# A group-normalised convolution with two kinds of image: where half products, sums and their transfers stand

## The chip, the core and the metric

The kernel runs on one core of a Trainium2 chip. The metric is the device time of one execution in microseconds; the number compared is the median over runs. The core has five engines with queues of their own that work in order: TensorE (PE: matmuls, PEld: its weight loads), VectorE (DVE), ScalarE (ACT), GpSimd (POOL) and SyncE (SP, which only issues transfers). Transfers run on 16 DMA engines; those that SP issues are plain loads and stores, those that POOL issues here add to what lies at their destination.

## The reference

The input `x` holds 160 images of 128 channels and 32 x 32 pixels, the weights `U` are 5 rows of 147456 numbers. What is computed, cut to what matters:

```python
def reference(x, L0_conv_U):
    def _L0_conv_ref(x, U):                       # N = 5 weight sets, 3 x 3 taps, padding 1
        s1 = (jnp.max(U) - jnp.min(U)) / 3.0
        v1 = s1 * floor(U / s1)
        s2 = s1 / 5.0
        v2 = s2 * floor((U - v1) / s2)
        w = (v1 + v2).reshape(128 * 5, 128, 3, 3)
        xb = x.reshape(B // 5, 5 * C, H, W)
        act = conv_general_dilated(xb, w, ..., feature_group_count=5)
        return act.reshape(...)
    def _gn(v, G=32, eps=1e-5):                   # 4 neighbouring channels form a group
        m, s = mean and variance of a group in one image
        return (v - m) / sqrt(s + eps)
    return x + _L0_conv_ref(_gn(x), L0_conv_U)
```

So each image is normalised by group of channels, convolved with one of five quantised 3 x 3 kernels, and added to itself. 32 images share a weight set.

## The kernel before

**Images and loops.** The 128 channels lie on the 128 partitions, so an image is a tile of 128 x 1024 f32 (512 KB). Two images form a chunk (`xt`), one load or one store of 1 MB. `Main.run` has one loop over the 160 images, and the order in which Python emits instructions is the order of every engine's queue (`tc.manual_schedule()`): nothing is reordered afterwards. In iteration `i` the convolution of image `i` is emitted, and beside it work for neighbouring images: statistics for image `i + 14`, normalised parts for `i + 2` to `i + 4`, the result of `i - 1`, the store of `i - 2` and loads that run up to 17 images ahead.

**Statistics.** `measure` makes two passes of ACT over an image: `image_sum` (L187) adds its values up, `image_square` (L196) adds up the squares of its deviations, with the negative mean as its bias. Between them POOL turns the sum into the negative mean `minus` (L189) and the mean in `mv` (L190), and after the second pass into the variance in `mv` (L199). Groups of eight images (smaller ones at the start) then share two small matmuls that average over channels (`means`, L205, and `variances`, L220), with POOL's arithmetic between (`deviations`, L213 to L217) and after them (`deviation` and `scales`, L226 to L238), which ends in `rstd`, `shift` and `twice`. The two matmuls are emitted by `on_the_way`, from inside the convolution of the two images after the one whose measuring completed the group.

**Two kinds of image.** The normalised image goes to PE as a sum of two f16 parts. A *plain* image has `z` (ACT, L486), its high part `hi` (ACT, L494) and the rest `lo` (DVE, L543). The high part is convolved tap by tap: 18 matmuls with up to 512 columns (`taps`, L583). For the low part pairs of rows are combined first (DVE, L556 to L559, tile `rows`), which needs fewer products: 12 matmuls of about 256 columns into `eo` and 6 of about 512 into `m` (`product`, L619). A *combined* image (every third one, `i % 3 == 2`, from 14 on, 48 in all) combines rows before it is split: DVE and POOL make `v` (`combine`, L515 to L525), ACT its high part `vh` (L530), DVE the low part `vl` (L536), and both go through `product` alone.

**From products to result.** `m` holds half products of pairs of rows, `eo` the rest, each in PSUM; there are two buffers for `eo` and one for `m`. `leave` (ACT, L667) copies `m` out, to `mm` (f16) for a plain image and to `mw` (f32) for a combined one. `pairs` (DVE, L679 and L680) makes the sum and the difference of the halves: for a plain image in a tile `pq` of its own, for a combined image in a tile of the pool `sums`, which has three buffers. `residual` (DVE) adds `eo`: L703 writes a new tile of `sums` for a plain image, L699 adds to the tile that `pairs` has already taken for a combined one; it also frees the buffer of `eo`. `accumulate` (POOL, L716) then issues the transfer that adds the sum to the image in `xt`, in SBUF, and after it SP issues the store (L721). A buffer of `sums` is free again when that transfer has landed.

**Order within iteration `i`.** PE: the six matmuls for `m` come first, or after the first of the three columns of taps where image `i - 1` is combined (`late`); `on_the_way` stands ahead of the last column. DVE: `low_combined(i + 1)`, `combine(i + 2)`, `residual(i - 1)`, `pairs(i)`, then `low_part(i + 2)` and `combinations(i + 2)`, and in 21 of the 32 iterations of each of the first four sets two steps of `make_column`, which builds the next set's weights. ACT: `normalise`, first pass, `leave(i)`, `high_part` or `high_combined`, second pass. POOL: its part of `combine`, the small operations of the statistics, and `accumulate(i - 1)` at the iteration's end. SP: the store of a finished chunk and then the loads, in order; a chunk's place is one of 11 (`xpool`).

## Time and profile before

| what | value |
|---|---|
| median of 3 runs | 1152.48 us (1145.69, 1152.48, 1153.7) |
| the profiled execution's own time | 1146.97 us |
| its span (first to last instruction) | 1145.2 us |
| mean granted TensorE clock | 0.975 of full speed |
| instructions | 16411 |
| DMA | 254.45 MB, mean 222 GB/s |
| accumulating transfers (`xt<-sum`) | 153 of 512 KB, median 7.1 us from issue to landing |

How to read it: the profile is one execution, in microseconds from the span's start. A row of the waits says which engine sat idle at which line, what ended the idle time, for how long in total, how often, and at most. The chain of waits follows the last instruction back, at each step to what released it. Lines such as L679 are lines of the kernel before. Tiles are named without their buffer's number, so `sum` stands for all buffers of that pool. In the kernel with the change every line below the first edit has moved by five or so (L679 is L684 there).

### The profile page before, as it was taken

The numbers are of one execution on the slowest core, as the hardware profiler recorded it, in microseconds if no ns is written. First come the engines' busy times: TensorE is split into PE (matmuls) and PEld (weight loads), VectorE is DVE, ScalarE is ACT, GpSimd is POOL, SyncE is SP. The second block draws the span as 40 slices with busy tenths as digits, with TensorE's granted clock in tenths as the row PEclk, the third lists the DMA queues.
The fourth block names the chain that finished last, engine by engine and source line by source line (L and its number), as shares of the span: only waits on it lengthen the run. The fifth ranks groups of instructions, "written<-read, shape, count | busy, mean of one in ns | idle before, by whom it ended". The sixth has DMA issues, their size and how long they took to land.

```text
span 1145.2 us, 16411 instructions
## 1 busy us (share of the span) xinstructions
PE 1023.7 (89%) x5910; PEld 582.4 (51%) x5910; DVE 962.7 (84%) x1363; ACT 841.9 (74%) x1137; POOL 596.4 (52%) x965
## 2 busy tenths in 40 slices
PE   1999797999889989898889999989988999998997
PEld 0455454555554546455446455545554555555554
DVE  7996698978788989787988977889978988877886
ACT  4799776778768868688677767777867887786541
POOL 4644555474456556555556565536555655463420
PEclk9999999999998999999989999999999999999999
DMA  9348697888997897899788889888879789987773
GB/s 364 127 133 243 158 237 205 221 228 230 269 251 199 222 254 202 224 264 239 217 221 221 221 227 244 226 211 237 232 208 237 223 237 243 249 247 202 180 202 132
DMA packets 67290, 254.45 MB, mean 222 GB/s; under 512 B 5248, under 2 KB 5248, under 8 KB 67200
## 3 DMA queue, kind: packets, MB, share of 16 engines
q1 hardware_dynamic: 45168, 173.09, 44.1%
q0 software_dynamic: 22032, 80.23, 36.7%
q8 instruction: 48, 0.79, 0.3%
q14 instruction: 42, 0.34, 0.1%
HBM read 89.19 MB, written 83.89 MB: 151 GB/s over the span
## 4 chain that ended last, share of the span: by engine, by line
ACT 21%; DMA 18%; POOL 18%; PE 17%; DVE 13%; issue 12%; SPq 0%; POOLq 0%; DVEq 0%; ACTq 0%
DMA xt<-sum 15%; PE eo L583 8%; ACT junk L187 4%; ACT vh L530 4%; PE m L619 4%; ACT junk L196 4%; PE eo L619 4%; ACT z L486 4%; DMA xt<-in_x_dram 3%; POOL mv L199 3%; POOL v L516 3%; POOL rstd L229 2%; POOL xt L716 2%; DVE lo L543 2%; ACT hi L494 2%
## 5 line engine op out<-in xcount | busy, mean ns | idle before, releaser
L583 PE MATMUL eo<-hi,wt 128*128 128x496 f16 (+3 forms) x1998 | 497.1, 387 | 57.4 <-DVE sum L699 55.9
L619 PEld LDWEIGHTS <-wt 128*128 128x128 f16 x3690 | 363.2, 99 | 253.5 <-issue 31.7
L583 PEld LDWEIGHTS <-wt 128*128 128x128 f16 x2070 | 206.9, 101 | 266.1 <-issue 83.9
L199 POOL TENSOR_SCALAR mv<-squares 128x1 f32<-128x1 f32 x157 | 105.3, 671 | 324.6 <-ACT junk L196 323.0
L530 ACT ACTIVATE vh<-v,rstd 128x2048 f16<-128x2048 f32 x48 | 96.1, 2002 | 148.6 <-DVE v L525 100.3
L619 PE MATMUL eo<-rows,wt 128*128 128x248 f16 (+1 forms) x1308 | 201.6, 278 | 0.0
L196 ACT ACTIVATE junk<-xt,minus 128x1024 f16<-128x1024 f32 x157 | 179.8, 1146 | 13.9 <-POOL minus L189 12.3
L187 ACT ACTIVATE junk<-xt 128x1024 f16<-128x1024 f32 x157 | 164.7, 1049 | 34.1 <-DMA xt<-in_x_dram 32.6
L619 PE MATMUL m<-rows,wt 128*128 128x496 f16 (+1 forms) x654 | 159.6, 380 | 18.6 <-ACT mm L667 7.1
L716 POOL DMA_DIRECT2D xt<-sum x153 | 137.8, 903 | 40.7 <-DVE sum L699 19.1
L486 ACT ACTIVATE z<-xt,shift,rstd 128x1024 f32<-128x1024 f32 x112 | 137.9, 1231 | 25.5 <-POOL shift L236 25.5
L667 ACT ACTIVATE mm<-m 128x1024 f16<-128x1024 f32 x109 | 110.1, 1010 | 47.8 <-PE m L619 47.7
L543 DVE TENSOR_TENSOR lo<-z,hi 128x1024 f16<-128x1024 f32 x112 | 136.6, 1220 | 1.0 <-ACT hi L494 1.0
L703 DVE SCALAR_TENSOR_TENSOR sum<-pq,eo 128x1024 f32<-128x1024 f16 x105 | 127.4, 1214 | 0.0
L536 DVE SCALAR_TENSOR_TENSOR vl<-v,rstd,vh 128x2048 f16<-128x2048 f32 x48 | 112.7, 2349 | 11.6 <-ACT vh L530 11.6
L679 DVE TENSOR_TENSOR sum<-mw 128x512 f32<-128x512 f32 x48 | 33.5, 697 | 99.7 <-DMA xt<-sum 60.3
L619 PE MATMUL m<-vh,wt 128*128 128x496 f16 (+1 forms) x288 | 110.6, 384 | 6.6 <-ACT mm L667 6.6
L494 ACT CAST hi<-z 128x1024 f16<-128x1024 f32 x112 | 116.0, 1036 | 0.1
L189 POOL TENSOR_SCALAR minus<-total 128x1 f32<-128x1 f32 x157 | 83.3, 530 | 61.9 <-ACT junk L187 60.7
L619 PE MATMUL m<-vl,wt 128*128 128x496 f16 (+1 forms) x288 | 110.6, 384 | 0.0
L619 PE MATMUL eo<-vl,wt 128*128 128x248 f16 (+1 forms) x576 | 110.2, 273 | 0.0
L619 PE MATMUL eo<-vh,wt 128*128 128x248 f16 (+1 forms) x576 | 110.1, 273 | 0.0
(114 smaller groups left out, 1194.6 us busy)
## 6 DMA issues: line engine op xcount, KB each, us to landing
xt<-in_x_dram SPq DMA_DIRECT2D x78, 1024.0 KB, 8.6
out_dram<-xt SPq DMA_DIRECT2D x78, 1024.0 KB, 5.0
xt<-sum POOLq DMA_DIRECT2D x153, 512.0 KB, 7.1
range<-in_L_conv_U_dram SPq DMA_DIRECT2D x4, 576.0 KB, 8.2
u<-in_L_conv_U_dram SPq DMA_DIRECT2D x4, 576.0 KB, 7.3
xt<-in_x_dram SPq DMA_DIRECT2D x4, 512.0 KB, 10.5
out_dram<-xt SPq DMA_DIRECT2D x3, 512.0 KB, 3.2
u<-in_L_conv_U_dram SPq DMA_DIRECT2D x2, 288.0 KB, 3.0
```

The costliest lines, as they stand in the source:

```text
L187: nc.scalar.activation(junk, image, ACTF.Copy, accum_out=total)
L196: nc.scalar.activation(junk, image, ACTF.Square, bias=self.minus[j], accum_out=squares)
L199: nc.gpsimd.tensor_scalar_mul(self.mv[:, j, 1:2], squares, 1.0 / image.shape[1])
L486: nc.scalar.activation(z, self.image(i), ACTF.Identity, bias=st.shift[:, j : j + 1], scale=st.rstd[:, j : j + 1],)
L494: self.nc.scalar.copy(hi.rearrange("p h w -> p (h w)"), self.z[i])
L530: self.nc.scalar.mul(vh, self.v[i], st.rstd[:, j])
L536: self.nc.vector.scalar_tensor_tensor(vl, self.v[i], st.rstd[:, j], self.hi[i], ALU.mult, ALU.subtract)
L543: self.nc.vector.tensor_sub(lo[:, 1 : self.H + 1, :].rearrange("p h w -> p (h w)"), self.z.pop(i), self.hi[i].rearrange("p h w -> p (h w)"),)
L583: nc.tensor.matmul(target[:, h, r0 - h0 : r1 - h0, c0:c1], self.wts[n, col][:, k, :], tile[:, s0 : s0 + r1 - r0, c0 + dw : c1 + dw], start ...
L619: nc.tensor.matmul(target[:, :, c0:c1], self.wts[n, col][:, kind, :], source[:, :, c0 + dw : c1 + dw], start=start, stop=stop,)
L703: nc.vector.scalar_tensor_tensor(self.sum[i], self.m.pop(i), 0.5 / UP, eo, ALU.mult, ALU.add)
L716: self.nc.gpsimd.dma_start(self.image(i), self.sum.pop(i), accum_op=ALU.add)
```

## The change

It does six things. (1) **Statistics:** both passes of ACT write straight into `mv`, the first with the scale -1/1024 (so `mv` holds the negative mean, which is the second pass's bias), the second as a plain sum of squares; POOL's three operations for each image go, one multiplication for each group of images is added on POOL (L220), two for each of three images are added on DVE, and the factor 1/1024 is applied once for each group on ACT. (2) **Half products** of a combined image get one tile of their own, `pqw`, in the pool `wide`; `residual` takes the tile of `sums`. (3) **`accumulate(i - 1)`** follows `residual(i - 1)` directly, instead of standing at the iteration's end. (4) **Orders:** where image `i` is combined, `pairs(i)` comes after `low_part(i + 2)` and `combinations(i + 2)`; where image `i - 1` is combined, the second pass follows the first, ahead of `leave(i)`. (5) **`on_the_way`** stands ahead of the second column of taps, and ahead of the late sums of pairs. (6) **Buffers:** 12 places for chunks instead of 11, one buffer for `vh` instead of two.

```diff
--- before.py
+++ after.py
@@ -159,11 +159,13 @@
+    size = 1024
     def __init__(self, nc, small, psum, gavg, mhalf, nb, scale, name):
         self.nc, self.small, self.psum, self.gavg, self.mhalf = nc, small, psum, gavg, mhalf
         self.nb, self.scale, self.name = nb, scale, name
         self.mv = self.tile("mv", [nb, 2])
-        self.minus = {}
     def tile(self, tag, shape):
         return self.small.tile(
@@ -178,25 +180,26 @@
         )
         for h in range(2):
             self.nc.vector.bn_stats(st[:, h, :], image[:, h * half : (h + 1) * half])
-        self.nc.vector.bn_aggr(self.mv[:, j, :], st)
+        both = self.tile("both", [2])
+        self.nc.vector.bn_aggr(both, st)
+        self.nc.vector.tensor_scalar_mul(self.mv[:, j, 0:1], both[:, 0:1], -1.0)
+        self.nc.vector.tensor_scalar_mul(
+            self.mv[:, j, 1:2], both[:, 1:2], float(image.shape[1])
+        )
     def image_sum(self, j, image, junk):
-        nc = self.nc
-        total = self.tile("total", [1])
-        nc.scalar.activation(junk, image, ACTF.Copy, accum_out=total)
-        minus = self.minus[j] = self.tile("minus", [1])
-        nc.gpsimd.tensor_scalar_mul(minus, total, -1.0 / image.shape[1])
-        nc.gpsimd.tensor_scalar_mul(self.mv[:, j, 0:1], total, 1.0 / image.shape[1])
+        self.nc.scalar.activation(
+            junk, image, ACTF.Copy, scale=-1.0 / image.shape[1],
+            accum_out=self.mv[:, j, 0:1],
+        )
     def image_square(self, j, image, junk):
-        nc = self.nc
-        squares = self.tile("squares", [1])
-        nc.scalar.activation(
-            junk, image, ACTF.Square, bias=self.minus[j], accum_out=squares
-        )
-        nc.gpsimd.tensor_scalar_mul(self.mv[:, j, 1:2], squares, 1.0 / image.shape[1])
+        self.nc.scalar.activation(
+            junk, image, ACTF.Square, bias=self.mv[:, j, 0:1],
+            accum_out=self.mv[:, j, 1:2],
+        )
     def means(self):
         self.pg = self.psum.tile(
@@ -208,11 +211,13 @@
     def deviations(self):
         nc, mv = self.nc, self.mv
         self.ngm = self.tile("ngm", [self.nb])
-        nc.scalar.mul(self.ngm, self.pg[:, 0, :], -1.0)
+        nc.scalar.copy(self.ngm, self.pg[:, 0, :])
         self.dv = self.tile("dv", [self.nb])
-        nc.gpsimd.tensor_tensor(self.dv, mv[:, :, 0], self.ngm, ALU.add)
+        nc.gpsimd.tensor_tensor(self.dv, mv[:, :, 0], self.ngm, ALU.subtract)
+        nc.gpsimd.tensor_scalar_mul(self.dv, self.dv, self.size**0.5)
         nc.gpsimd.tensor_tensor(self.dv, self.dv, self.dv, ALU.mult)
         nc.gpsimd.tensor_tensor(self.dv, self.dv, mv[:, :, 1], ALU.add)
@@ -223,7 +228,7 @@
         nc = self.nc
         ve = self.tile("ve", [self.nb])
-        nc.scalar.copy(ve, self.pg[:, 1, :])
+        nc.scalar.mul(ve, self.pg[:, 1, :], 1.0 / self.size)
         nc.gpsimd.tensor_scalar_add(ve, ve, EPS)
         self.rstd = self.tile("rstd", [self.nb])
         nc.gpsimd.tensor_tensor(self.rstd, ve, self.mhalf[:, : self.nb], ALU.pow)
@@ -349,12 +354,12 @@
         self.qpool = pool("quant", 1)
         self.wpool = pool("weights", 2)
         self.upool = pool("u", 1)
-        self.xpool = pool("x", 11)
+        self.xpool = pool("x", 12)
         self.zpool = pool("z", 3)
         self.parts = pool("parts", 4)
         self.rows = pool("rows", 4)
         self.wide = pool("wide", 1)
-        self.wide_parts = pool("wide_parts", 2)
+        self.wide_parts = pool("wide_parts", 1)
         self.evac = pool("evac", 2)
         self.sums = pool("sums", 3)
         self.unread = pool("unread", 1)
@@ -639,10 +644,10 @@
             sums_of_pairs()
         eo = self.eo[i] = self.banks(self.ps_eo, "eo", i)
         for col in self.COLS:
-            if late and col == self.COLS[1]:
-                sums_of_pairs()
-            if col == self.COLS[-1]:
+            if col == self.COLS[1]:
                 on_the_way()
+                if late:
+                    sums_of_pairs()
             if not combined:
                 self.taps(i, (self.hi[i], 0), col, eo, False)
             for a, kind in enumerate((0, self.MINUS_G2)):
@@ -672,7 +677,7 @@
         nc = self.nc
         m = self.m.pop(i).rearrange("p a (i w) -> p a i w", w=self.W)
         if self.combined(i):
-            pq = self.sums.tile([self.P, 1024], F32, tag="sum", name=f"sum{i}")
+            pq = self.wide.tile([self.P, 1024], F32, tag="pq", name=f"pqw{i}")
         else:
             pq = self.evac.tile([self.P, 1024], MM, tag="pq", name=f"pq{i}")
         rows = pq.rearrange("p (i a w) -> p i a w", a=2, w=self.W)
@@ -694,12 +699,11 @@
         eo = self.eo.pop(i).rearrange("p h r w -> p (h r w)")
         del self.hi[i]
         n, b = self.place(i)
-        if self.combined(i):
-            self.sum[i] = self.m.pop(i)
-            nc.vector.tensor_add(self.sum[i], eo, self.sum[i])
-            return
         if not self.by_hand(i):
             self.sum[i] = self.sums.tile([self.P, 1024], F32, tag="sum", name=f"sum{i}")
+            if self.combined(i):
+                nc.vector.tensor_add(self.sum[i], eo, self.m.pop(i))
+                return
             nc.vector.scalar_tensor_tensor(
                 self.sum[i], self.m.pop(i), 0.5 / UP, eo, ALU.mult, ALU.add
             )
@@ -874,9 +878,11 @@
                 self.combine(i + 2)
             for k in parted:
                 self.normalise(k)
+            stages = (0, 1) if self.combined(i - 1) else (0,)
             for k in to_measure:
                 if not self.by_vector(k):
-                    self.measure(k, (0,))
+                    self.measure(k, stages)
             if i >= self.FIRST:
                 self.leave(i)
             for k in parted:
@@ -889,11 +895,15 @@
                     self.combinations(i + 2)
             if i > self.FIRST:
                 self.residual(i - 1)
-            if i >= self.FIRST:
+                self.accumulate(i - 1)
+            if i >= self.FIRST and not self.combined(i):
                 self.pairs(i)
             if self.STEADY <= i + 2 < self.imgs and not self.combined(i + 2):
                 self.low_part(i + 2)
                 self.combinations(i + 2)
+            if self.combined(i):
+                self.pairs(i)
             for st in middle:
                 st.deviation()
                 st.scales()
@@ -901,7 +911,8 @@
                 st.deviations()
             middle, ready = ready, []
             for k in to_measure:
-                self.measure(k, (1,))
+                if self.by_vector(k) or 1 not in stages:
+                    self.measure(k, (1,))
                 group = self.group_of[k]
                 if k + 1 == self.groups[group].stop:
                     ready.append(self.stats[group])
@@ -913,7 +924,6 @@
                 take(later, 2)
                 if b == self.per_set - 1:
                     run(later)
-            self.accumulate(i - 1)
             self.store(i - 2)
             while loaded * NB < min(self.imgs, i + self.LOAD_LEAD):
                 self.load(loaded)
```

DVE around combined image 59 (image 58 and 60 are plain, `v62` belongs to the next combined one), before:

```order
L703 SCALAR_TENSOR_TENSOR sum58_4840<-pq58_4768,eo58_4718 128x1024
L679 TENSOR_TENSOR sum59_4842<-mw59_4836 128x16x32
L680 TENSOR_TENSOR sum59_4842<-mw59_4836 128x16x32
L543 TENSOR_TENSOR lo1_171<-z61_4753,hi61_4764 128x1024
L556 TENSOR_TENSOR rows61_4846<-lo1_171 128x1024
L558 TENSOR_TENSOR rows61_4846<-lo1_171 128x512
L559 TENSOR_TENSOR rows61_4846<-lo1_171 128x512
L519 TENSOR_TENSOR v62_4904<-xt31_3910 128x960
L522 SCALAR_TENSOR_TENSOR v62_4904<-xt31_3910,twice10_4279 128x512
L525 TENSOR_TENSOR v62_4904<-xt31_3910 128x512
L699 TENSOR_TENSOR sum59_4842<-eo59_4802,sum59_4842 128x1024
L679 TENSOR_TENSOR pq60_4921<-mm60_4916 128x16x32
```

and now:

```order
L707 SCALAR_TENSOR_TENSOR sum58_4452<-pq58_4386,eo58_4339 128x1024
L548 TENSOR_TENSOR lo1_171<-z61_4374,hi61_4381 128x1024
L561 TENSOR_TENSOR rows61_4456<-lo1_171 128x1024
L563 TENSOR_TENSOR rows61_4456<-lo1_171 128x512
L564 TENSOR_TENSOR rows61_4456<-lo1_171 128x512
L684 TENSOR_TENSOR pqw59_4460<-mw59_4448 128x16x32
L685 TENSOR_TENSOR pqw59_4460<-mw59_4448 128x16x32
L524 TENSOR_TENSOR v62_4514<-xt31_3592 128x960
L527 SCALAR_TENSOR_TENSOR v62_4514<-xt31_3592,twice10_3939 128x512
L530 TENSOR_TENSOR v62_4514<-xt31_3592 128x512
L705 TENSOR_TENSOR sum59_4528<-eo59_4418,pqw59_4460 128x1024
L684 TENSOR_TENSOR pq60_4531<-mm60_4524 128x16x32
```

What moved: the pairs of image 59 stand behind the low part of image 61, they write `pqw59`, and `sum59` is first written by image 59's residual (L705), where before the pairs (L679) had taken its buffer nine rows ahead of that residual.

POOL from the shift of a group of images to the transfer of image 59's sum (`mv`, `minus`, `squares`: statistics of images 73 and 74), before:

```order
L236 TENSOR_TENSOR shift11_4856<-ngm11_4776,rstd11_4853 128x8
L238 TENSOR_SCALAR twice11_4858<-ngm11_4776 128x8
L199 TENSOR_SCALAR mv12_4755<-squares12_4861 128x1
L716 DMA xt29_3606<-sum58_4840 128x1024
L515 TENSOR_SCALAR v62_4904<-xt31_3910,ngm10_4181 128x32
L516 TENSOR_SCALAR v62_4904<-xt31_3910,ngm10_4181 128x32
L189 TENSOR_SCALAR minus12_4913<-total12_4911 128x1
L190 TENSOR_SCALAR mv12_4755<-total12_4911 128x1
L199 TENSOR_SCALAR mv12_4755<-squares12_4925 128x1
L716 DMA xt29_3606<-sum59_4842 128x1024
```

and now, from the transfer of image 58's sum to that of 59:

```order
L720 DMA xt29_3311<-sum58_4452 128x1024
L232 TENSOR_SCALAR ve11_4463<-ve11_4463 128x8
L234 TENSOR_TENSOR rstd11_4466<-ve11_4463,mhalf_167 128x8
L238 TENSOR_SCALAR rstd11_4466<-rstd11_4466,lift_116 128x8
L241 TENSOR_TENSOR shift11_4469<-ngm11_4394,rstd11_4466 128x8
L243 TENSOR_SCALAR twice11_4471<-ngm11_4394 128x8
L520 TENSOR_SCALAR v62_4514<-xt31_3592,ngm10_3843 128x32
L521 TENSOR_SCALAR v62_4514<-xt31_3592,ngm10_3843 128x32
L720 DMA xt29_3311<-sum59_4528 128x1024
```

What moved: the transfer of image 58's sum stood behind the group's last operations and a second pass's result, and now stands ahead of the group's operations; that of image 59's sum stood behind the results of both passes of image 74, which are gone, and now follows POOL's part of `v62` directly.

PE inside the convolution of plain image 66, which follows a combined one (`wt2_1`, `wt2_0`, `wt2_2`: the three columns of taps in the order in which they are used), before:

```order
L619 LDWEIGHTS wt2_0_4195
L619 MATMUL eo66_5265<-rows66_5188,wt2_0_4195 128x8x31
L205 MATMUL pg12_5293<-mv12_4755,gavg_163 128x8
L583 LDWEIGHTS wt2_2_4702
L583 MATMUL eo66_5265<-hi66_5047,wt2_2_4702 128x16x31
```

and now:

```order
L624 LDWEIGHTS wt2_1_3389
L624 MATMUL eo66_4841<-rows66_4773,wt2_1_3389 128x8x32
L208 MATMUL pg12_4852<-mv12_4376,gavg_163 128x8
L624 LDWEIGHTS wt2_1_3389
L624 MATMUL m66_4854<-rows66_4773,wt2_1_3389 128x512
```

What moved: the group's small matmul on `mv12` stood behind the second column, with the six matmuls for `m66` long done, and now stands behind the first column and ahead of `m66`.

## Prediction

> **What bounds the kernel now.** The page first, then the waits of all engines, then the chain of waits through one slow stretch, then single stretches.
>
> ```profile
> core 0: 1145.2 us, clock 0.975
> PE 1023.7 (89%) x5910; PEld 582.4 (51%) x5910; DVE 962.7 (84%) x1363; ACT 841.9 (74%) x1137; POOL 596.4 (52%) x965
> DMA xt<-sum 15%; PE eo L583 8%; ACT junk L187 4%; ACT vh L530 4%; PE m L619 4%; ACT junk L196 4%; PE eo L619 4%; ACT z L486 4%; DMA xt<-in_x_dram 3%; POOL mv L199 3%; POOL v L516 3%; POOL rstd L229 2%; POOL xt L716 2%; DVE lo L543 2%; ACT hi L494 2%
> ```
>
> PE is the busiest engine, yet the largest single piece of the chain is not PE but the accumulating transfer, 15%. The waits say who is waiting for it:
>
> ```profile
> POOL mv L199 <- ACT junk L196: 323.0, 115, 11.2
> ACT vh L530 <- DVE v L525: 100.3, 24, 7.8
> DVE sum L679 <- DMA xt<-sum: 60.3, 18, 6.1
> PE eo L583 <- DVE sum L699: 55.9, 25, 3.5
> DVE sum L679 <- ACT mw L667: 37.0, 22, 3.8
> ACT junk L187 <- DMA xt<-in_x_dram: 32.6, 11, 11.8
> ACT z L486 <- POOL shift L236: 25.5, 11, 3.8
> PE m L619 <- ACT mm L667: 13.7, 8, 4.8
> ```
>
> The third row is the pairs of a combined image, waiting for a buffer of `sums`; the fourth is PE, waiting for the residual behind those pairs. The chain shows both in one piece, and the timeline how it reaches PE:
>
> ```profile
> 656.95 1.89 POOL mv L199
> 658.83 10.59 DMA xt<-sum
> ...
> 669.52 0.71 DVE sum L679
> ...
> 675.80 2.00 ACT vh L530
> ```
>
> ```profile
> 675.62 1.22 DVE L699 TENSOR_TENSOR sum<-eo,sum 128x1024 f32<-128x1024 f32 x1
> 676.90 2.07 PE L583 MATMUL eo<-hi,wt 128*128 128x512 f16 x6 [2.33 <-DVE sum L699]
> ```
>
> A transfer issued only once POOL got past L199 lands 10.59 us later; then L679 runs, and all of DVE that is queued behind it (low part, `v`, L699) is late, so ACT's `vh` is late and PE stands for 2.33 us. It costs more than the wait: after such a stall PE can run at half clock. The stretches (span, busy time of PE, PEld, DVE, ACT, POOL, then granted clock, DMA share, GB/s) show it in the first row, after a stall of 3.40 us; then a stretch with a late transfer, and two from one `mw` to the next without:
>
> ```profile
> 593.00:600.00 7.00, 6.90 (x23) 3.04 (x23) 6.92 (x10) 7.00 (x9) 3.50 (x4) 0.57 0.53 162
> 664.00:689.00 25.00, 22.14 (x132) 12.96 (x131) 17.30 (x23) 16.27 (x25) 15.22 (x25) 0.93 0.84 226
> 645.20:664.10 18.90, 18.90 (x118) 11.34 (x117) 18.70 (x27) 15.63 (x21) 9.11 (x14) 1.00 0.88 244
> 1073.50:1091.60 18.10, 18.10 (x111) 10.60 (x110) 14.99 (x21) 9.13 (x9) 2.97 (x5) 1.00 0.84 195
> ```
>
> Three images (one combined) take 18.1 us where PE alone is the limit, 18.9 us where DVE also builds weights (it is busy 18.70 of them), and 25 with a late transfer. `mw` is copied once in three images:
>
> ```profile
> L667 ACT ACTIVATE mw<-m x48: 997/1007/1025, 145.6 to 1109.6; 128x1024 f32<-128x1024 f32 x48
> ```
>
> 47 periods in 1109.6 - 145.6 = 964.0 us, 20.5 us on average.
>
> **The change, part by part.** *Half products in their own place, and transfers issued with their sums.* Before, the pairs of image i took the buffer of image i-3's sum, whose transfer was issued at the end of iteration i-2, behind L199: little over one iteration (a third of 20.5, so 7 us) for a transfer that takes
>
> ```profile
> DMA to landing us min/median/max: 4.5/7.1/11.6
> ```
>
> Now the buffer is taken by the residual of image i, in iteration i+1, and the transfer of image i-3 follows its own residual: three iterations, 18 us at the fast period. Against 11.6 us at most, the 60.3 us of waiting go. The next thing late would be `mw`, the fifth row of the waits; it loses its hold on DVE too, since a low part now stands ahead of the pairs. Moved ahead of POOL's statistics, the transfer makes the group's operations wait for a DVE residual; they have the rest of an iteration. SP's stores wait for these transfers, so stores and then loads are earlier, and with the twelfth place the 32.6 us of waiting for `x` should go as well; they are part of the slow periods, so I do not add them.
>
> *What the periods then come to.* By the code, weights are built in 24 of the 47 periods: 24 x 18.9 + 23 x 18.1 = 869.9, which is 94.1 us less than 964.0. That is the gain if every period becomes a fast one.
>
> A rule bears on the clock in this. The Trainium skill, TensorE: Matmul & The Clock Gate, Part 1, says that the clock falls to half after at least one idle window of about 3.4 us; here the stall of 2.33 us at 676.90 was enough (0.93 in its stretch), so the measurement decides. By the rule hardly any stall here (longest 3.5) would cost clock, and the gain would be smaller by the clock's whole deficit, at most 0.025 x 1145.2 = 28.6 us; by the rows that deficit is inside the 94.1, so the rule gets no chance of its own.
>
> *Statistics without POOL.* Gone from POOL are, for each of 157 images, an L199, an L189 and its twin L190:
>
> ```profile
> L199 POOL TENSOR_SCALAR mv<-squares 128x1 f32<-128x1 f32 x157 | 105.3, 671 | 324.6 <-ACT junk L196 323.0
> L189 POOL TENSOR_SCALAR minus<-total 128x1 f32<-128x1 f32 x157 | 83.3, 530 | 61.9 <-ACT junk L187 60.7
> L196 ACT ACTIVATE junk<-xt,minus 128x1024 f16<-128x1024 f32 x157 | 179.8, 1146 | 13.9 <-POOL minus L189 12.3
> ```
>
> About 270 us of work, and 323.0 us in which POOL stood at L199 with the transfers queued behind it. POOL is at 52%, so the work itself is worth nothing; its worth is in the term above and in the 12.3 us of ACT. ACT's passes keep their length. The added multiplication (once for a group, 0.67 us by the row of L199) lies on the way to `z` and is part of the bounds of that wait below; DVE's six small ones at the start are taken as 0.
>
> *The second pass ahead of `leave`.* It puts 1.15 us more in front of `mm` in one of three iterations. ACT stood there for the matmuls anyway:
>
> ```profile
> 609.55 1.02 ACT L667 ACTIVATE mm<-m 128x1024 f16<-128x1024 f32 x1 [1.35 <-PE m L619]
> ```
>
> so nothing while ACT is on time. Where it is late, each costs PE 1.2 us (PE's wait for `mm`: 13.7 us in 8). I keep 10 us of that wait as staying; bounds 0 and 48 x 1.2 = 58.
>
> *`z` waiting for `shift`* (25.5 us) hangs on the order `ve`, POOL's chain, `z`, which the change leaves alone. Half of it reaches PE, I take it: 12, between 0 and 25.5.
>
> *`on_the_way` earlier.* It stands ahead of a column of taps, and in a late image ahead of `m` too:
>
> ```profile
> 608.05 1.46 PE L619 MATMUL m<-rows,wt 128*128 128x512 f16 x6
> 609.35 1.43 PE L583 MATMUL eo<-hi,wt 128*128 128x496 f16 x6
> 610.62 0.60 PE L619 MATMUL eo<-rows,wt 128*128 128x248 f16 x4
> 611.06 1.44 PE L583 MATMUL eo<-hi,wt 128*128 128x496 f16 x6
> ```
>
> 1.30 us for `m` and 1.71 for a column, so 1.7 or, in a late image, 3.0 us earlier. Its slack now, in two groups (end of the second pass to L205; L217 to L220):
>
> ```profile
> 448.80 0.19 ACT L196 ACTIVATION_READ_ACCUMULATOR junk<-xt,minus 128x1 f32 x1
> 451.17 0.29 PE L205 MATMUL pg<-mv,gavg 128*128 128x8 f32 x2
> 398.96 0.65 POOL L217 TENSOR_TENSOR dv<-dv,mv 128x8 f32<-128x8 f32 x1
> 401.24 0.29 PE L220 MATMUL pg<-dv,gavg 128*128 128x8 f32 x2
> ```
>
> 2.2 us and 1.6 us: some of these matmuls, and all of PE behind them, will wait. For the 18 full groups I take 0.5 us each: 9, between 0 and 18 x 2 = 36.
>
> *One buffer for `vh`* costs nothing: its next writer comes an iteration after the matmuls that read it.
>
> **The sum.** 94.1 - 10 - 12 - 9 = 63.1 us. The profiled execution took 1146.97 (1.8 more than its span), so 1083.9 on its level; the median of the runs lies 5.5 above it and one run of three below, so I add half: **1087**. With the kept terms at nothing it is 1087 - 31 = 1056; with `shift` and `on_the_way` at their upper bounds 1087 + 13.5 + 27 = 1127. The forecast's own range is 1062 to 1112.
>
> **The rivals.** *ACT takes the transfer's place.* DVE waited at L679 for `mw` in 22 cases and for the transfer in 18. If ACT is late in those 18 too, half of PE's 55.9 us and half of the clock's 28.6 stay and only 42 go: 1105 on the profiled level, 1108. For it: the `vh` row (100.3 us). Against: that wait is for `v`, so DVE made ACT late, and in the fast stretches ACT is busy 15.63 of 18.90.
>
> *The DMA engines become the bound.* Three images move nine times 512 KB, 4.72 MB. Over 100 us and over 20 us the most is
>
> ```profile
> 900.00:1000.00 100.00, 95.78 (x574) 55.81 (x573) 82.86 (x111) 81.28 (x109) 56.27 (x92) 1.00 0.91 245
> 498.00:518.00 20.00, 20.00 (x126) 12.06 (x125) 15.86 (x21) 14.63 (x21) 13.76 (x22) 1.00 0.99 277
> ```
>
> 277 GB/s gives 17.0 us for a period, below 18.1. But if no more than 235 can be kept up (about midway from the table's mean of 222 to 245), a period takes 20.1: 47 x 20.1 = 945, 19 us saved, 1131. Against it: the 277 was reached with PE busy all the time. A rule speaks for it: the Trainium skill, DMA: Bandwidth & Descriptors, under Issuing engines are not separate DMA queues, says that transfers of all issuers share the 16 engines and interleave, so an earlier issue buys no bandwidth; the 0.99 above agrees that they can be full.
>
> *Slower: PE stands at the statistics.* L205 and L220 stand in PE's queue 36 times for the full groups. Where ACT and POOL run as late behind PE as now, an earlier place is a wait of PE, and of 2.3 us or more it also costs clock. The point from which the gain is eaten is 72.1 (63.1 and the 9 charged) / 36 = 2.0 us each; at 3.0 us each it is 1087 - 9 + 108 = 1186. For it: the slack of 1.6 to 2.2 us. Against: without POOL's L199 the input of L205 is there sooner, by 1.89 us in the chain above, and only the places in late images move by 3.0.
>
> *The change doesn't reach it.* Transfers are still held back on POOL, by weights and `v`, and the buffers still come late: within 1% of now, 1150.
>
> **Chances.** Forecast 0.68, ACT 0.16, DMA 0.10, PE at the statistics 0.04, no effect 0.02. A measurement of this kernel tells about 1% from no change (the three runs spread over 0.7%). The forecast, 0.15 of ACT's and 0.07 of DMA's case are faster by over 1%: 0.90; the rest of these two, at smaller gains, and no effect are 0.06; slower 0.04. The range is 1062 to 1124.
>
> **What would show it.** Right: the wait of DVE for `xt<-sum` under 10 us, that of PE for the combined residual under 15, the clock at 0.99, `mw` to `mw` at 18 to 19.5 us throughout, DMA at 240 GB/s or more over the span. The first term is wrong if DVE now waits for `xt<-sum` at the residuals; the second if PE's wait for `mm` grows; the `on_the_way` term if PE waits at L208 and L225 for over 30 us. DMA is the bound if ACT's wait for `x` grows.

## The result and the profile after

| | before | after |
|---|---|---|
| median of the runs | 1149.09 us (1145.3 to 1153.7, 4 runs) | 1060.77 us (1059.38 to 1062.11, 4 runs) |
| the profiled execution, its span | 1146.97, 1145.2 us | 1060.39, 1058.6 us |

The ratio is 0.923, 95% interval 0.9184 to 0.9275: 7.7% faster. The forecast was 1087 with a range from 1062, so the kernel came out 26 us below the forecast and just below its range. Three lines of the page of after (span and clock, busy times, the chain by line):

```profile
core 0: 1058.6 us, clock 0.995
PE 999.6 (94%) x5910; PEld 577.4 (55%) x5910; DVE 961.4 (91%) x1369; ACT 846.2 (80%) x1137; POOL 395.8 (37%) x517
PE 25%; DVE 7%; issue 3%; POOL 3%; DMA 2%; ACT 1%; SPq 0%; POOLq 0%; ACTq 0%
```

PE is busy in 94% of the span instead of 89%, at a clock of 0.995 instead of 0.975. The chain of after could be followed back only to 617 us, so its shares add up to 41% of the span, where those of before add up to 99%, and the two don't compare one to one. In the part that was followed PE leads, with 25 of the 41, and all transfers have 2; before, transfers had 18 of 99. The waits of after (in all, times, longest), the rows that answer to those of before:

```profile
POOL xt L720 <- DVE sum L707: 296.0, 82, 8.0
ACT vh L535 <- DVE v L530: 36.0, 19, 3.0
POOL dv L219 <- ACT ngm L217: 34.3, 9, 12.8
ACT z L491 <- POOL shift L241: 31.8, 12, 5.4
PE pg L225 <- POOL dv L222: 20.9, 11, 4.9
ACT junk L192 <- DMA xt<-in_x_dram: 17.4, 8, 10.7
PE m L624 <- ACT mm L672: 6.2, 6, 2.2
PE eo L588 <- DVE sum L705: 2.8, 7, 0.5
DVE pqw L684 <- ACT mw L672: 1.6, 3, 0.5
```

VectorE's wait for the transfer (60.3 us before) is in no row any more; its wait for `mw` fell from 37.0 to 1.6, PE's for the combined residual from 55.9 to 2.8, ACT's for `v` from 100.3 to 36.0. Of the rows of PE, ACT and VectorE shown here two grew: PE at L225 (7.4 before), where the second small matmul of the statistics waits for the deviations, and the wait for `shift` (25.5 before). POOL's 296.0 us (10.9 before) is a queue that stands in an issued transfer until the sum is there; it costs nothing by itself, but what is queued behind it waits as well. The row of `mw`, once in three images:

```profile
L672 ACT ACTIVATE mw<-m x48: 999/1023/1026, 141.7 to 1022.7; 128x1024 f32<-128x1024 f32 x48
```

47 periods in 1022.7 - 141.7 = 881.0 us, 18.74 each instead of 20.51. That is 83.0 of the 86.6 us that the span lost; the start gave 3.9 (145.6 to 141.7). Three stretches of after (span, busy time of PE, PEld, DVE, ACT, POOL, then clock, DMA share, GB/s):

```profile
349.70:367.75 18.05, 18.05 (x110) 10.56 (x109) 17.88 (x27) 15.84 (x20) 4.64 (x5) 1.00 0.89 253
858.50:876.70 18.20, 18.20 (x112) 10.72 (x111) 15.84 (x22) 15.79 (x21) 6.33 (x10) 1.00 1.01 272
761.40:785.20 23.80, 20.56 (x116) 11.32 (x114) 23.29 (x33) 16.62 (x26) 13.51 (x19) 0.93 0.95 258
```

In the first, weights are built (DVE is busy 17.88 of 18.05) and yet PE alone sets the length: the 18.9 us that the prediction took for such periods is no floor. The third is one of four periods still above 22 us, where the prediction had 18 to 19.5 throughout. What holds it, in one piece of the timeline of after:

```profile
770.96 1.22 DVE L705 TENSOR_TENSOR sum<-eo,pqw 128x1024 f32<-128x1024 f32 x1
771.14 2.00 ACT L535 ACTIVATE vh<-v,rstd 128x2048 f16<-128x2048 f32 x1 [2.85 <-DVE v L530]
772.48 0.89 POOL L720 DMA_DIRECT2D xt<-sum  x1 [5.38 <-DVE sum L705]
773.05 0.14 ACT L217 COPY ngm<-pg 128x8 f32<-128x8 f32 x1
773.28 0.82 POOL L219 TENSOR_TENSOR dv<-mv,ngm 128x8 f32<-128x8 f32 x1
773.97 2.34 DVE L541 SCALAR_TENSOR_TENSOR vl<-v,rstd,vh 128x2048 f16<-128x2048 f32 x1
774.20 2.21 POOL L220 TENSOR_SCALAR dv<-dv 128x8 f32<-128x8 f32 x1
776.76 0.20 POOL L222 TENSOR_TENSOR dv<-dv,mv 128x8 f32<-128x8 f32 x1
777.02 0.39 PE L225 MATMUL pg<-dv,gavg 128*128 128x8 f32 x2 [2.92 <-POOL dv L222]
```

ACT copies the means (`ngm`) only behind `vh`, which waits for `v`; POOL's arithmetic on them follows, and PE stands for 2.92 us.

### The profile page after: what moved, and what is told of

The parts are those of the page before. It is cut to its first block, busy times and chain, and to the rows that moved or that the text cites. A ratio compares the mean times of both kernels' runs of the same rounds, so it can differ in the third digit from the quotient of the medians.

```text
span 1058.6 us, 15880 instructions
## 1 busy us (share of the span) xinstructions
PE 999.6 (94%) x5910; PEld 577.4 (55%) x5910; DVE 961.4 (91%) x1369; ACT 846.2 (80%) x1137; POOL 395.8 (37%) x517
## 5 line engine op out<-in xcount | busy, mean ns | idle before, releaser
L588 PE MATMUL eo<-hi,wt 128*128 128x496 f16 (+3 forms) x1998 | 482.3, 378 | 5.4 <-DVE sum L705 2.8
L720 POOL DMA_DIRECT2D xt<-sum x153 | 134.8, 881 | 546.5 <-DVE sum L707 296.0
L624 PE MATMUL eo<-rows,wt 128*128 128x248 f16 (+1 forms) x1308 | 197.6, 274 | 0.0
L199 ACT ACTIVATE junk<-xt,mv 128x1024 f16<-128x1024 f32 x157 | 180.7, 1151 | 1.8
L192 ACT ACTIVATE junk<-xt 128x1024 f16<-128x1024 f32 x157 | 164.8, 1050 | 18.9 <-DMA xt<-in_x_dram 17.4
L491 ACT ACTIVATE z<-xt,shift,rstd 128x1024 f32<-128x1024 f32 x112 | 138.1, 1233 | 31.8 <-POOL shift L241 31.8
L707 DVE SCALAR_TENSOR_TENSOR sum<-pq,eo 128x1024 f32<-128x1024 f16 x105 | 127.5, 1215 | 5.3 <-PE eo L624 5.3
L672 ACT ACTIVATE mw<-m 128x1024 f32<-128x1024 f32 x48 | 48.9, 1018 | 52.1 <-PE m L624 51.9
L684 DVE TENSOR_TENSOR pq<-mm 128x512 f16<-128x512 f16 x109 | 45.7, 419 | 41.0 <-ACT mm L672 40.8
L561 DVE TENSOR_TENSOR rows<-lo 128x1024 f16<-128x1024 f16 x109 | 76.2, 699 | 3.7
```

The source lines that it names most:

```text
L192: self.nc.scalar.activation(junk, image, ACTF.Copy, scale=-1.0 / image.shape[1], accum_out=self.mv[:, j, 0:1],)
L199: self.nc.scalar.activation(junk, image, ACTF.Square, bias=self.mv[:, j, 0:1], accum_out=self.mv[:, j, 1:2],)
L491: nc.scalar.activation(z, self.image(i), ACTF.Identity, bias=st.shift[:, j : j + 1], scale=st.rstd[:, j : j + 1],)
L588: nc.tensor.matmul(target[:, h, r0 - h0 : r1 - h0, c0:c1], self.wts[n, col][:, k, :], tile[:, s0 : s0 + r1 - r0, c0 + dw : c1 + dw], start ...
L624: nc.tensor.matmul(target[:, :, c0:c1], self.wts[n, col][:, kind, :], source[:, :, c0 + dw : c1 + dw], start=start, stop=stop,)
L672: self.nc.scalar.mul(m, self.m.pop(i).rearrange("p a i w -> p a (i w)"), scale)
```

## The experiments

B stands for the buffers and transfers (own place, transfers issued with their sums), S for the statistics without POOL, O for the orders (pairs, second pass, `on_the_way`). Each run is given as its median and its ratio to before with the 95% interval. The theory at the outset was that of the prediction: B is what makes the periods fast, S and O matter little. The rival: S or O carries a good part. The runs were taken at several times; the median of before moved between 1148.8 and 1152.0 us from one to the next, so a difference of 3 to 4 us between two kernels is no larger than that.

**B in its parts.** In the kernel before, `e3_own_place`:

```diff
-            pq = self.sums.tile([self.P, 1024], F32, tag="sum", name=f"sum{i}")
+            pq = self.wide.tile([self.P, 1024], F32, tag="pq", name=f"pqw{i}")
...
-        if self.combined(i):
-            self.sum[i] = self.m.pop(i)
-            nc.vector.tensor_add(self.sum[i], eo, self.sum[i])
-            return
...
+            if self.combined(i):
+                nc.vector.tensor_add(self.sum[i], eo, self.m.pop(i))
+                return
```

> The kernel before with one part of the change: half products of combined images in a tile of their own, the buffer of sums taken by the residual. Theory (the late buffer of sums is what made three images take 20.5 us): the buffer is needed over two iterations after its transfer is issued, about 13 us against a landing of 4.5 to 11.6, so most of the wait of DVE for the transfer (60.3 us) goes, and with it PE's wait for the combined residual and the clock: 1085 to 1100 us. Rival (the statistics on POOL are what costs, because the transfers stand behind them): 1130 us or more, with the wait for the transfer now at the residuals.

`e4_transfer_early`, also in the kernel before:

```diff
                 self.residual(i - 1)
+                self.accumulate(i - 1)
...
-            self.accumulate(i - 1)
             self.store(i - 2)
```

> The kernel before with one part of the change: the transfer of a sum issued right behind its residual, everything else as before. Theory: the buffer is still taken by the pairs, but its transfer is issued most of an iteration earlier, so about two thirds of the wait goes: 1100 to 1120 us. Rival (only the place of the half products matters): no change, 1140 us or more.

`e5_place_and_transfer` is both.

> The kernel before with both, the tile of its own and the early transfer; statistics, orders and the other buffers as before. Theory (one cause, removed twice): within 8 us of the better of the two alone, 1080 to 1095 us, the rest down to 1061 being the statistics and the orders. Rival (the two add up): 1065 us or less, nothing left for the other parts.

Measured: 1106.33 (0.9606, 0.9549 to 0.9662), 1093.77 (0.9496, 0.9442 to 0.955) and 1092.15 (0.9479, 0.9424 to 0.9534). Either one removes VectorE's wait for the transfer. The own place gave a little less than expected, the early transfer alone more, nearly all that both do together. With the own place alone ACT waits 54.6 us at `vh` for POOL's part of `v` (24.5 with the early transfer); why the transfer's place matters there was not followed up. But the two together leave 31 us to after. The waits of the run with both:

```profile
ACT vh L530 <- DVE v L525: 61.9, 23, 3.3
DVE pqw L679 <- ACT mw L667: 48.2, 27, 4.6
ACT z L486 <- POOL shift L236: 29.5, 11, 4.4
PE eo L583 <- DVE sum L700: 24.6, 22, 2.4
PE m L619 <- ACT mm L667: 13.6, 11, 3.3
```

With the transfer out of the way, `mw` holds VectorE instead (48.2, before 37.0), what is queued behind the pairs is late, and PE still stands 24.6 us for the combined residual: the "next thing late" of the prediction, not yet relieved.

**Single parts taken out of after.** `e6_statistics_back` gives POOL its three operations for each image again, all else as in after:

```diff
-            junk, image, ACTF.Copy, scale=-1.0 / image.shape[1],
-            accum_out=self.mv[:, j, 0:1],
+        nc.scalar.activation(junk, image, ACTF.Copy, accum_out=total)
+        nc.gpsimd.tensor_scalar_mul(minus, total, -1.0 / image.shape[1])
+        nc.gpsimd.tensor_scalar_mul(self.mv[:, j, 0:1], total, 1.0 / image.shape[1])
...
+        nc.gpsimd.tensor_scalar_mul(self.mv[:, j, 1:2], squares, 1.0 / image.shape[1])
```

> The changed kernel with the statistics of the kernel before, three operations of POOL for each image. With the buffers alone the kernel came to 1092 us, so some 31 us of the gain are due to other parts. Theory (the order of the combined pairs and of the second pass carries these): POOL is no bound, so 1061 to 1068 us. Rival (the statistics carry them, since ACT's second pass and the transfers wait for POOL): 1078 us or more, with ACT waiting for POOL at the second pass and at vh.

1102.39 (0.9574, 0.9512 to 0.9636): the theory that POOL's operations were worth nothing beyond the transfers fell, they cost 42 us here. Two waits:

```profile
ACT junk L196 <- POOL minus L189: 122.9, 52, 5.6
POOL xt L715 <- DVE sum L702: 95.5, 76, 5.3
```

ACT stood 122.9 us for the negative mean (12.4 with B alone): in after's order the second pass follows the first at once, so the scaling between them is no longer covered, and it is queued on POOL behind transfers that wait for sums. PE's wait for `mm` rises with it, from 6.2 to 36.1 us. `e8_second_pass_back` puts only the second pass behind `leave`, `e10_stats_and_pass_back` puts back both:

```diff
-            stages = (0, 1) if self.combined(i - 1) else (0,)
+            stages = (0,)
```

> The changed kernel with the second pass of the statistics always behind leave. Theory (that order only fills idle time of ACT, and the time lost is that of vh coming 1.2 us later or earlier): 1060 to 1068 us. Rival (ahead of leave it delays mm and with it PE): faster than the changed kernel, 1055 us or less.

> After, with the statistics' small operations back on GpSimd and also the second pass over an image back behind the departing image, everywhere. With the statistics alone put back the time was 1102.4, with the second pass alone put back 1067.3. Theory: GpSimd's scalings cost what they do because in after the second pass stands right behind the first one, so that nothing covers the scalings between (ScalarE waited 122.9 us for them); with the departing image in between they are covered again, and the two edits together cost less than their sum: 1070 to 1085. Rival: GpSimd's scalings are late wherever they stand, because they are queued behind transfers that wait for VectorE's sums: 1098 to 1112, with ScalarE's wait for the minus still over 80 us.

1067.3 (0.9277, 0.9218 to 0.9337) and 1071.25 (0.9302, 0.9256 to 0.9347). The second pass by itself is worth 6.5 us. With the old place of the pass POOL's operations cost 4 us, with the new place 42: the price of S hangs on this order, as the theory had it.

`e7_pairs_back` puts the pairs of a combined image ahead of the low part again:

```diff
-            if i >= self.FIRST and not self.combined(i):
+            if i >= self.FIRST:
                 self.pairs(i)
...
-            if self.combined(i):
-                self.pairs(i)
```

> The changed kernel with the pairs of a combined image back ahead of the low part. Theory (with the buffers alone DVE still stood 48 us at these pairs, waiting for mw, and the combined residual behind them kept PE waiting 25 us): both come back, 1075 to 1090 us. Rival (DVE has the time to wait): 1061 to 1066 us, with the wait for mw but without PE's.

1077.19 (0.9358, 0.9298 to 0.9417), 16 us slower than after. Its waits show the same row as B alone:

```profile
ACT vh L535 <- DVE v L530: 61.6, 36, 3.1
DVE pqw L684 <- ACT mw L672: 50.8, 26, 3.9
```

So it is the low part ahead of the pairs that takes `mw`'s hold on VectorE away (1.6 in after). PE's wait for the combined residual, which the theory had coming back too, rose only from 2.8 to 5.2 us; what rose besides is its wait for the deviations (20.9 to 27.3) and for `mm` (6.2 to 8.8), and the clock fell to 0.991. How the 16 us come about in PE is thus not the way that the theory had it. `e9_buffers_back` has 11 chunk places and two `vh` buffers:

```diff
-        self.xpool = pool("x", 12)
+        self.xpool = pool("x", 11)
...
-        self.wide_parts = pool("wide_parts", 1)
+        self.wide_parts = pool("wide_parts", 2)
```

> The changed kernel with 11 places for chunks and two buffers for vh. Theory (with the transfers issued early the stores and loads are in time with 11 places as well, and vh is not waited for): 1060 to 1064 us. Rival (the twelfth place is what keeps ACT from waiting for x): 1070 us or more, with ACT's wait for x up from 17 us to 35 or more.

1060.63 (0.9213, 0.9153 to 0.9272): nothing. ACT's wait for `x` is 19.2 us (17.4 in after, 32.6 before), so it was not the twelfth place that brought it down. `e1_variances_late` leaves the means ahead of the second column and puts the variances' matmul back ahead of the last:

```diff
-                on_the_way()
+                on_the_way(0)
                 if late:
                     sums_of_pairs()
+            if col == self.COLS[-1]:
+                on_the_way(1)
```

> The changed kernel with the second small matmul of the statistics (the variances) back ahead of the last column of taps; the first one stays ahead of the second column. Theory (that matmul now stands in PE's queue before its input is there, 16 us with the clock lost behind it): PE's waits for dv go, 1045 to 1052 us. Rival (what comes later at PE comes later at shift too, and the stall moves to z and from there to PE): 1058 to 1066 us, with ACT's wait for shift up by 10 us or more.

1056.33 (0.9166, 0.9113 to 0.9219), between the ranges of the two views: PE's wait for the deviations is halved (20.9 to 11.6 us), ACT's for `shift` is up by 4.4 us, and the earlier place costs some 4 us.

**The parts alone and in pairs.** `e11_buffers_and_stats` is B and S, `e16_statistics_alone` S, `e17_orders_alone` O, `e18_statistics_and_orders` S and O, all made from before with the edits of the change's diff.

> The kernel before with the half products in a place of their own, the transfers issued right behind their sums (1092.2 with these two alone) and the statistics without GpSimd; the orders of before stay. Theory: the second pass of before stands behind the departing image, where the scalings are covered, but GpSimd's queue is held by the early transfers, so that the statistics still pay a little: 1078 to 1088, and the orders by kind of image give the remaining 20 to 25 us. Rival: the statistics give most of what is left, as the 42 us lost by putting them back into after suggest: 1062 to 1072.

> The kernel before with the statistics without GpSimd and nothing else: the half products stay in the place of the sums, the transfers at the iteration's end, the orders as before. Theory: without the operation that stood ahead of the transfers for 323 us, these are issued earlier, so that part of what the own place gives is had already: 1105 to 1125. Rival: the transfers are held by other things (the weights, the end of the iteration) and the statistics give only the 12 to 15 us that they give next to the buffers: 1132 to 1142.

> The kernel before with the orders of after and nothing else: the pairs of a combined image behind the low part, the second pass ahead of the departing image behind a combined one, the two small matmuls ahead of the second column. Theory: the orders are worth something only once statistics and transfers are off the path; here the adjacent passes wait for GpSimd's scalings and the pairs still wait for the transfer: 1140 to 1165, no gain or a loss. Rival: the later pairs alone relieve the wait for the transfer, and the orders give 20 to 40 us: 1112 to 1132.

> After without what the prediction rests on: the half products of a combined image again in the place of a sum, the transfers at the iteration's end, 11 chunk places and two buffers for vh; statistics and orders as in after. Theory: each of the three parts lets the transfer land before the pairs need its place, and the three overlap, so that the own place and the early transfers are worth little on top of the other two: 1060 to 1072. Rival: the own place gives its share in any company, 30 us or more: 1090 to 1110.

| in the kernel | us | ratio, 95% |
|---|---|---|
| B | 1092.15 | 0.9479 (0.9424 to 0.9534) |
| S | 1095.95 | 0.9533 (0.9467 to 0.9599) |
| O | 1117.04 | 0.9726 (0.9656 to 0.9796) |
| B and S | 1077.63 | 0.9359 (0.9314 to 0.9405) |
| B and O (`e6_statistics_back`) | 1102.39 | 0.9574 (0.9512 to 0.9636) |
| S and O | 1067.51 | 0.9287 (0.9259 to 0.9314) |
| all: after | 1060.77 | 0.923 (0.9184 to 0.9275) |

S alone gave about as much as B alone, more than either view expected; next to B it gives 14.5 us, at the edge of what the theory of that run had (1078 to 1088). O alone gave 34 us, as its rival said. S and O without B are within 7 us of after, as the theory said. The parts overlap, because each of them lets the transfer land before the pairs need its place. VectorE's wait for it and the row that stays, first with S alone, then with O alone:

```profile
ACT vh L535 <- DVE v L530: 91.3, 34, 5.8
DVE sum L684 <- ACT mw L672: 34.0, 24, 3.7
PE eo L588 <- DVE sum L704: 26.6, 20, 3.2
DVE sum L684 <- DMA xt<-sum: 15.8, 5, 3.5
```

```profile
ACT junk L196 <- POOL minus L189: 141.1, 57, 6.9
PE m L619 <- ACT mm L667: 48.2, 34, 4.6
DVE sum L679 <- DMA xt<-sum: 7.8, 4, 4.1
```

60.3 us of waiting for the transfer are 15.8 with S (L199 no longer stands ahead of the issue) and 7.8 with O (the pairs ask later). With S, `mw` still holds VectorE; with O, the uncovered scalings hold ACT, and PE waits 48.2 us for `mm`. Little is left of these where S and O come together: 1.3 us for the transfer, 1.6 for `mw`, 6.1 for `mm`.

**What the statistics still cost.** `e12_shift_later` does POOL's power twice in each group, with the same result:

```diff
         nc.gpsimd.tensor_tensor(self.rstd, ve, self.mhalf[:, : self.nb], ALU.pow)
+        nc.gpsimd.tensor_tensor(self.rstd, ve, self.mhalf[:, : self.nb], ALU.pow)
```

> After, with GpSimd's power done twice in each group, with the same result, so that the shift of each of the groups comes later by the duration of one such operation (0.2 to 2 us). Theory: the shift's wait lies in ScalarE's spare time and reaches TensorE in few places, so that the time grows by no more than 4 us, to 1060 to 1065. Rival: the wait for the shift stands on the path, as the prediction charged with half of 25.5 us: each of some 16 groups passes on its whole delay, 10 to 20 us, 1070 to 1081.

`e14_short_chain` takes an operation out of that chain:

```diff
-        nc.scalar.mul(ve, self.pg[:, 1, :], 1.0 / self.size)
-        nc.gpsimd.tensor_scalar_add(ve, ve, EPS)
+        nc.scalar.activation(
+            ve, self.pg[:, 1, :], ACTF.Identity, bias=self.mhalf[:, -1:], scale=1.0 / self.size
+        )
```

> After, with the epsilon of the variance added on ScalarE in the copy of the variances (its bias), so that GpSimd's addition (0.87 us on average, and 0.8 us of idle time ahead of it, for each group) goes from the chain that ends in the shift. Theory: doubling the power made the chain longer by 39 us in 23 groups and the time by 15 to 17, so about 0.4 of the chain's length reaches TensorE; the chain is shorter by 20 to 35 us here, and the time falls by 8 to 14, to 1047 to 1053. Rival: the shift is in time in after and late only when delayed, so that shortening gives nothing: 1058 to 1063.

1077.48 (0.9368, 0.9321 to 0.9415) and 1060.32 (0.9218, 0.9155 to 0.928). The longer chain costs 17 us, the shorter gives nothing. The added power took 39.1 us in 23 groups, and ACT's wait for `shift` rose from 31.8 to 58.6:

```profile
ACT z L492 <- POOL shift L242: 58.6, 18, 6.6
```

The shorter chain took the wait for `shift` only to 27.2. Both times lie in the ranges of the rivals; the theory of e14, that the price of lengthening also holds for shortening, was wrong. This fits a shift that comes just in time in after, so that its wait lies in time that ACT has to spare and a longer one does not. That reading is not shown to be the only one: the added power also holds POOL's queue, and ACT's wait for POOL's part of `v` rose from 9.3 to 16.0 us, PE's for `mm` from 6.2 to 11.4 and for the deviations from 20.9 to 24.0. Which of these carry the 17 us was not separated.

`e2_ngm_early` copies the means ahead of `leave` in the iterations behind a combined image; `e13_transfer_behind_stats` besides issues a transfer behind the statistics' operations of its iteration; `e15_best` does so only behind a combined image and where the deviations are due, and has the late variances of e1 and the short chain of e14:

```diff
+            for st in ready if self.combined(i - 1) else ():
+                st.copy_means()
             if i >= self.FIRST:
                 self.leave(i)
...
-                self.accumulate(i - 1)
+                behind = bool(ready) and self.combined(i - 1)
+                if not behind:
+                    self.accumulate(i - 1)
...
+            if i > self.FIRST and behind:
+                self.accumulate(i - 1)
             middle, ready = ready, []
```

(e13 has the condition `not ready and not middle` for the transfer's old place. In e14 and e15 a ninth column of `mhalf` holds the epsilon.)

> After, with ScalarE's copy of the means (ngm) issued ahead of the departing image in the iterations behind a combined image, where after issues it behind, in ScalarE's queue behind the copy vh that waits for the sum v. Theory: what is left of the long periods (23.61, 22.65, 22.35 and 23.79 us, with TensorE's waits of 2.1 to 2.9 us for the deviations and the stretch of low clock behind them) comes from that place in the queue, so that TensorE's waits for the deviations fall from 20.9 us in all to under 10, the four periods to about 20 us, and the time by 8 to 14 us, to 1047 to 1053. Rival: the copy only moves the wait, since vh starts later by as much and the parts made of it are late for TensorE instead: 1057 to 1064, with the wait of ScalarE's vh unchanged or larger and a new wait of TensorE for the parts.

> After, with the copy of the means early as in the run before (which alone moved nothing), and with the transfer of an image issued behind the statistics' operations of its iteration, where there are any, where after issues it ahead of them. Theory: GpSimd's queue stood in that transfer, waiting for VectorE's sum up to 8 us, and this is what holds the statistics: TensorE's waits for the deviations fall from 20.6 us to under 10, the long periods (21.65, 23.07, 23.61) to under 20.5, the time to 1046 to 1054. Rival: these waits come from ScalarE's and VectorE's queues and not from GpSimd's, and the later transfers cost as much as they give: 1057 to 1066.

> After, with four small things together: the small matmul of the variances back ahead of the last column (alone 1056.3), the means copied early, the transfer behind the statistics' operations only in the iterations behind a combined image, and the epsilon added on ScalarE (alone nothing). Theory: what holds the long periods is the deviations being late for that matmul, by ScalarE's copy and by GpSimd's transfer in those iterations only; with both out of the way and the matmul 1.7 us later its wait goes to nearly nothing, 1048 to 1054. Rival: in those iterations the deviations come out of one queue as late as out of the other, and only the later matmul counts: 1055 to 1059.

Measured: 1061.11 (0.9212, 0.9166 to 0.9257), 1058.65 (0.9191, 0.9128 to 0.9254), 1048.81 (0.9119, 0.9092 to 0.9146). The first moved the wait, though not to where its rival had it. Its timeline at the same place:

```profile
771.71 0.14 ACT L214 COPY ngm<-pg 128x8 f32<-128x8 f32 x1
777.37 0.90 POOL L723 DMA_DIRECT2D xt<-sum  x1 [5.38 <-DVE sum L708]
777.98 1.01 POOL L221 TENSOR_TENSOR dv<-mv,ngm 128x8 f32<-128x8 f32 x1
781.92 0.39 PE L227 MATMUL pg<-dv,gavg 128*128 128x8 f32 x2 [2.92 <-POOL dv L224]
```

The means are there at 771.71, and POOL does not take them up before 777.98, because the transfer ahead in its queue waits 5.38 us for VectorE. PE's wait is 2.92 us, unchanged. Moving every such transfer (e13) frees the deviations, and PE's wait falls to 8.7 us, as its theory had it, but the time stays in the range of its rival. That ACT now waits 31.9 us for `x` instead of 17.4 may be what takes the gain back; it is not shown:

```profile
ACT junk L192 <- DMA xt<-in_x_dram: 31.9, 16, 11.1
PE pg L227 <- POOL dv L224: 8.7, 6, 4.9
```

Moving only those behind a combined image, with the matmul a column later, gives the fastest kernel, 12 us below after, as its theory said:

```profile
core 0: 1048.8 us, clock 0.998
...
ACT z L496 <- POOL shift L244: 27.4, 12, 3.7
ACT junk L192 <- DMA xt<-in_x_dram: 24.8, 14, 12.3
PE m L629 <- ACT mm L679: 7.3, 8, 2.8
PE pg L227 <- POOL dv L224: 2.2, 1, 2.2
...
L679 ACT ACTIVATE mw<-m x48: 999/1020/1027, 142.1 to 1013.0; 128x1024 f32<-128x1024 f32 x48
```

PE's wait for the deviations is 2.2 us, and the clock is at 0.998. The four edits were not tried one by one in this company, so their shares of the 12 us are open beyond what e1 and e2 gave alone. The four long periods are still there, at 22.95, 22.05, 21.33 and 22.96 us; but the period behind each takes 15.7 us, where in after it takes 16.5 to 18.1. The four pairs together fall from 162.3 to 152.1 us, which is all that the 47 periods gain (881.0 to 870.9). So the length of a single period is a poor sign of lost time: what a long one costs shows only with the next.

## Why the forecast was 26 us too high, point by point

**The step that failed** is in the sum, 94.1 - 10 - 12 - 9: the waits for `mm` (10) and for `shift` (12) were kept as staying, and in after neither is seen to cost more than the 6.2 us in which PE stands for `mm`. Of the first term 83.0 us came, so that 11.1 us stayed behind where 31 were kept, and e15 shows what most of them were: late deviations, the matter of the third term. With PE's wait for these down to 2.2 us the 47 periods take 870.9 us, against the 869.9 of the first term, though ACT's wait for `shift` (27.4) and PE's for `mm` (7.3) are still there. That the two agree to a microsecond is in part luck, since periods of 15.7 to 23.0 us make up the 870.9. So 20 of the 26 us are terms kept too large, 3.9 are the start, and most of the rest is the level.

The account of what makes the periods fast failed as well, though the sum does not show it. The prediction put it to the transfer, with the statistics' worth "in the term above and in the 12.3 us of ACT" and the second pass at "nothing while ACT is on time". B alone gave 1145.2 - 1090.6 = 54.6 us of span; S on top of B gave 14.5 us by the medians, and O on top of both 16.9.

- *The transfer as the bound, and its wait gone:* right: the wait is gone with B, down to 15.8 us with S alone and to 7.8 with O alone. What would be late next, `mw`, was named rightly too, and the low part ahead of the pairs does relieve it; but its worth (16 us by e7) was not counted apart from B.
- *94.1 us if every period becomes fast:* 83.0 came. The 18.9 us for a period with weights is no floor (18.05 in the first stretch above), and against that stand the long periods, which were not in the picture; the 11.1 us are what is left of both.
- *`mm`, 10 us:* PE waits 6.2 us for it in all, less than before. The second pass ahead of `leave` was bounded by 0 and a loss of 58; it gains 6.5 us. The bound should have held a gain.
- *`shift`, 12 us:* the wait stayed (31.8 us), and neither shortening the chain (e14) nor the best kernel, with 27.4 us of the wait left, shows a cost. The longer chain costs 17 us (e12), so a wait and its price are not in proportion, and half of a wait was no way to price it.
- *`on_the_way`, 9 us:* the place costs 4 us (e1); e15, which takes away nearly all lateness of the deviations, gains 12 us. Right in size.
- *POOL:* that the group's operations behind the transfer "have the rest of an iteration" was wrong for the iterations behind a combined image, where the residual is late; that is the 5.38 us above.
- *Loads:* the 32.6 us of waiting for `x` "should go as well"; 17.4 stayed, and the twelfth place had no part in it (e9).
- *Rivals:* ACT did not take the transfer's place. DMA moved 240 GB/s over the span and was no bound, at up to 272 GB/s in a stretch where PE was busy throughout. PE did stand at the statistics, 20.9 us and not 108.
- *Level:* the median of after lies 0.4 us above the profiled execution, not half of 5.5; the start gave 3.9 us that the sum did not hold.

## What to carry to other kernels

Where several edits each shorten the wait for the same late thing, price them together and then one by one from the state that the others leave: here each alone gave 34 to 58 us, and all together 88. An order and a latency belong together: bringing two dependent passes next to each other was worth 6.5 us without POOL between them and cost 31 with it. An instruction that issues a transfer held its queue here until its data was there (5.38 us in the timelines above), so put behind a late producer only what nobody waits for.

## What the runs showed of the hardware

GpSimd's smallest operations have no fixed price. Of one line and tile (min, median, max in ns):

```profile
L220 POOL TENSOR_SCALAR dv<-dv x23: 221/592/2212, 20.7 to 970.1; 128x8 f32<-128x8 f32 x18, 128x4 f32<-128x4 f32 x3, 128x2 f32<-128x2 f32 x2
```

The longest, 2.21 us for 8 values in a partition, is the one in the timeline of after above: it begins at 774.20 and ends at 776.41, just behind VectorE's `vl` (773.97 to 776.31). The other two above 2 us (2.20 at 172.40 and 2.21 at 320.53) stand beside a `vl` as well, and the three that stand beside nothing but L707, which reads one of its inputs from PSUM, take 0.23 us each. The Trainium skill, SBUF — State Buffer, SBUF: two separate sides, says that VectorE and GpSimd share a pair of ports, and that of a VectorE instruction with two inputs from SBUF and a GpSimd one that reads SBUF the first to start has the pair for its whole length; `vl` reads two, and these rows agree.

The clock does not follow the length of a stall alone. In after PE stood 2.09 us at 323.36 and 2.72 us at 625.17; the stretches behind them:

```profile
323.00:330.00 7.00, 6.64 (x31) 3.44 (x32) 6.21 (x10) 2.95 (x7) 5.01 (x9) 0.76 0.77 197
625.00:640.00 15.00, 14.83 (x90) 8.86 (x91) 12.72 (x20) 11.89 (x17) 7.63 (x11) 1.00 0.85 219
```

The shorter stall cost clock (0.76), the longer one did not (1.00). So the 2.3 us from which the prediction took a stall to cost clock is no threshold; what decides was not found.
